# Attention's output norm in a macaron block: a head's inverse root as a zero-step stationary operand in four column groups, in place of a spread copy and its transposes

## The chip, the cores and the metric

The kernel runs on 1 core of one Trainium2 chip. The metric is the device time of one execution in microseconds (us), here the median of several runs. The engines are named as in the profile: PE is TensorE (PEld its weight loads), DVE is VectorE, ACT is ScalarE, POOL is GpSimd, SP is SyncE, which only issues transfers here.

## What is computed

A "macaron" block on x of shape (8, 512, 512), f32: half a feed-forward layer, attention, and half a feed-forward layer again. The feed-forward layer lets each of 16 experts choose its 256 best tokens; all experts share one 512x512 matrix. The attention has 16 heads of width 32 and 4 key heads, a second softmax over the difference of two, and a norm for each head. Cut to what matters:

```python
x = x + 0.5 * ffn(layernorm(x))
x = x + attn(layernorm(x))
x = x + 0.5 * ffn(layernorm(x))

def attn(x):
    ...
    diff = softmax(where(causal, NEG, scores[:, 0] - lam * scores[:, 1]))
    att = einsum('bhqv,bvhd->bqhd', diff, v)
    att = att * rsqrt(mean(att * att, axis=-1, keepdims=True) + EPS) * rms_w
    att = att * (1.0 - LAM_INIT)
    return att.reshape(b, s, E) @ Wo

def ffn(x):
    logits = xf @ router_w + router_b
    G, idx = top_k(softmax(logits, axis=-1).T, k)
    y = zeros.at[idx].add(G * (xf[idx] @ expert_w + expert_b))
    return y
```

The change is in the line with `rsqrt`: every token has 16 numbers, one for each head, and each must multiply the 32 values of its head.

## The kernel before, in words

The whole of x stays in SBUF, a batch of 512 tokens as four tiles of 128 tokens. The order of the work on every engine is written out by hand: each engine does its instructions in the order in which the program lists them, and waits only for what they need.

*Feed-forward, twice* (`ffn`, L213). A batch is normalised by POOL (`xn`, L254), transposed by PE (`tp`, L265), routed (`lgp`, L284, with the padded router weights `rwp` as a stationary operand of 32 columns in four column groups), and multiplied by the expert matrix (`yps`, L317); POOL adds the bias `eb` (L327). Then a search over 30 bits finds the threshold (`search`, L386, with the 0/1 masks `blk`, `low` and `seg`, which are slices of `sel`), and `update` (L451) adds the weighted result to x. Router weights, bias and masks are loaded once, at the start, into the pool `keep`, and are used by both layers.

*Attention* (`attention`, L460). For each batch there are two halves, `gp` 0 (called even here) and `gp` 1 (odd), and each half has 11 blocks: a block is a tile of 128 queries with some of the heads. The loop at L938 goes through all 176 blocks. In one turn `k` the engines work on five blocks at once: scores of block k+1 (`sc`, L655), energies with mask and row minimum (`e`, L672, on DVE), first exponentials (L685, on ACT), weights on POOL (`fac` L699, `e` L714, the causal fill L721) and the difference of the two softmaxes (`t`, L734, on DVE) for block k-1, second exponentials (L748) for k-2, transposes of `t` (`tp`, L768, copied out at L781 and L783), and the product with v for k-4 (`av`, L796, copied out at L811). The `av` matmuls have 32 stationary columns and stand at the column positions 0, 32, 64 and 96.

Beside the blocks, other work is put into *slots* of a turn: "short" and "long" for PE, "act mid" and "act" for ACT, "mid" and "dve" for DVE, "pool" for POOL. The pool slot comes last in a turn, and its first instruction waits for the difference `t` of that turn (L736). `plan` (L863) decides which work goes to which turn of a half:

- `norm_steps` (L467): in the even half of batch b, the norm of batch b+1. Statistics on DVE in turns 0 and 3, the inverse root on ACT in turn 4 (L480, L481), then on POOL the shift `nmr` = -mean x rstd as two instructions (L485, L486) and the normalised tile `h` (L488) in turns 6 to 9, the transposes `htp` (L496) in turns 7, 8 and 10. For batch 0 the same steps run before the blocks, while DVE still does the updates of the first feed-forward layer.
- `rope_steps` (L536): projections `r_ps` (L547) in turns 0 to 4, with two DVE instructions that read the PSUM bank (`r`, L556, and `r_by`, L558), two transfers on SP's queue for the swap (L564), and an addition on POOL (L568). `value_steps` (L515): `vps` (L523).
- `finish_steps` (L574): for each of a batch's four tiles, the head norm, the output projection and the residual. Tiles 0 and 1 are finished in the batch's odd half, tiles 2 and 3 in the next batch's even half, so 32 times in all.

The steps of `finish_steps`, with the turns of tiles 0, 1, 2 and 3 in their halves:

- POOL squares the attention output, `sq` (L583), and the second softmax's sum, `u` (L584); turns 4, 6, 0, 3.
- PE sums the squares over each head, `f_ss` (L590); DVE adds (L596); ACT takes the inverse root in two instructions (L601, L602). `u` then has 16 numbers for each of 128 tokens; turns 5, 7, 1, 5.
- POOL copies `u` out to 512 columns, each number 32 times, `f_ux` (L606); turns 5, 8, 1, 6.
- PE transposes it in four pieces into a PSUM bank, `f_f` (L614), and DVE multiplies with the attention output, `f_an` (L618); turns 7, 9, 4, 7.
- PE projects, `f_o` (L626), in turns 9, 10, 5, 8, and DVE adds to x (L632) a turn later.

`sq`, `f_ux` and `f_an` share two buffers of the tag "sq"; `h` has two buffers of its own. A new tile in a shared buffer waits until the last reader of the old one is through. The PSUM tiles of these steps, and `r_ps`, `vps`, `av` and `htp`, take turns in two banks (`MISC`).

In the last odd half (batch 7) there is no projection left; products of the second feed-forward layer take the "long" slots (`early_steps`, L888). Thirteen turns follow (`drain`, L1056), which finish tiles 2 and 3 of batch 7 beside that layer's first steps.

Of the kernel before, what the change touches and what calls it, by code (L numbers as in the profile page):

```python
# [9 lines left out]
F32 = mybir.dt.float32  # L10
I32 = mybir.dt.int32
AF = mybir.ActivationFunctionType
ALU = mybir.AluOpType
# [3 lines left out]
P = 128  # L17
B, S, E = 8, 512, 512
NT = B * S // P
TPB = S // P  # L20
EC = E // P
H, KVH, D = 16, 4, 32
R = H // KVH
NEXP = 16
# [9 lines left out]
C_BLK = C_SWAP + P  # L34
C_LOW = C_BLK + P
C_SEG = C_LOW + P
C_ALL = C_SEG + B
# [3 lines left out]
def macaron_kernel(  # L41
# [57 lines left out]
    eb_sb = keep.tile([P, E], F32, name="eb")  # L99
    sel = keep.tile([P, C_ALL - C_BLK], F32, name="sel")  # L100
    blk, low = sel[:, :P], sel[:, P : 2 * P]
    seg = sel[:, C_SEG - C_BLK : C_SEG - C_BLK + B]

    rwp = keep.tile([P, EC, 32], F32, name="rwp")
# [108 lines left out]
    def ffn(f):  # L213
# [5 lines left out]
        def new(kind, name, shape, dtype=F32, tag=None, **kw):  # L219
            return home[kind].tile(list(shape), dtype, name=f"{name}{f}", tag=tag or kind, **kw)  # L220

        def load():
            held["we"] = new("we", "we", [P, EC, E])
            nc.sync.dma_start(held["we"], expert_w.rearrange("(c p) n -> p c n", p=P))

# [53 lines left out]
        def logits_pe(b):  # L279

            lgps[b] = bank(at["lgp"], f"lgp{f}_{b}")
            xT = buf[b].rearrange("p i (c t) -> p c i t", c=EC)
            for c in range(EC):
                nc.tensor.matmul(  # L284
                    lgps[b][32 * c : 32 * (c + 1), :], rwp[:, c, :], xT[:, c], start=True,
                    stop=True, tile_position=(0, 32 * c),
                )
# [38 lines left out]
        def product_bias(b, i):  # L326
            return nc.gpsimd.tensor_tensor(buf[b][:, i, :], buf[b][:, i, :], eb_sb, ALU.add)  # L327
# [58 lines left out]
        def search(per_bit):  # L386

            softmax(1)
# [13 lines left out]
            thr = tiny.tile([P, 1], I32, name=f"thr{f}", tag="thr")  # L402
# [20 lines left out]
            cg = tiny.tile([P, 1], F32, name=f"cg{f}", tag="cg")  # L423
            ce = tiny.tile([P, 1], F32, name=f"ce{f}", tag="ce")
# [11 lines left out]
            need = tiny.tile([P, 1], F32, name=f"need{f}", tag="need")  # L436
# [11 lines left out]
            held["wt"] = tiny.tile([P, TPB, B], F32, name=f"wt{f}", tag="wt")  # L448
# [11 lines left out]
    def attention(f0, f1, home, first_end, projections_end, drain):  # L460
# [6 lines left out]
        def norm_steps(at, b, st):  # L467

            mv = tiny.tile([P, TPB, 2], F32, name=f"mv{b}", tag="a_mv")
            rstd = tiny.tile([P, TPB], F32, name=f"rstd{b}", tag="a_rstd")  # L470
            nmr = tiny.tile([P, TPB], F32, name=f"nmr{b}", tag="a_nmr")
# [10 lines left out]

            def apply(i):
                if i == 0:
                    nc.gpsimd.tensor_tensor(nmr, mv[:, :, 0], rstd, ALU.mult)  # L485
                    nc.gpsimd.tensor_scalar(nmr, nmr, -1.0, None, ALU.mult)  # L486
                hs[i] = home["h"].tile([P, E], F32, name=f"h{b}_{i}", tag="h", bufs=2)
                return nc.gpsimd.tensor_scalar(  # L488
                    hs[i], x_sb[b][:, i, :], rstd[:, i : i + 1], nmr[:, i : i + 1],
                    ALU.mult, ALU.add,  # L490
                )
# [21 lines left out]
            at(4, "act", scale)  # L513

# [59 lines left out]
        def finish_steps(at, os, b, i, st):  # L574
# [29 lines left out]
            def spread():  # L604
                t["ux"] = home["sq"].tile([P, 4, P], F32, name=f"{name}_ux", tag="sq", bufs=2)
                return nc.gpsimd.tensor_copy(  # L606
                    t["ux"].rearrange("p c (h d) -> p (c h) d", d=D),
                    t["u"].unsqueeze(2).to_broadcast([P, H, D]),
                )

            def turn():
                t["f"] = misc(f"{name}_f")
                for c in range(4):
                    nc.tensor.transpose(t["f"][:, c * P : (c + 1) * P], t["ux"][:, c, :], ident)  # L614
# [24 lines left out]
            at(o2, "pool", spread)  # L639
# [355 lines left out]
    CHOICE = ("st", "gt", "eq", "rank")  # L995
# [10 lines left out]
    nc.vector.memset(rwp, 0.0)  # L1006
    nc.sync.dma_start(rwp[:, :, :NEXP], router_w.rearrange("(c p) n -> p c n", p=P))
# [3 lines left out]
    nc.sync.dma_start(eb_sb, expert_b.partition_broadcast(P))  # L1011
    nc.sync.dma_start(sel, consts[:, C_BLK:])
# [19 lines left out]
    home = dict.fromkeys(("h", "hT", "kq0", "by", "sw"), proj)  # L1032
    opened = {}

    def first_end():
        first_y.close()
        opened["out"], opened["blocks"] = pool("out", "right"), pool("blocks", "right")
        home.update(dict.fromkeys(("aT", "sq"), opened["out"]))
        home.update(dict.fromkeys(("kq1", "v", "e", "t", "eT"), opened["blocks"]))

    def projections_end():
        proj.close()
        wpool.close()
        opened["early"] = pool("early", "left")
        f1.home.update(dict.fromkeys([*Y[:3], "we", *SMALL], opened["early"]))
        f1.at.update(tp=MISC, y=MISC, lgp=MISC, lg=MISC)
        f1.load()

    def blocks_end():
        opened["blocks"].close()  # L1050
        opened["late"] = pool("late", "right")
        f1.home.update(dict.fromkeys([*Y[3:], *CHOICE], opened["late"]))

# [107 lines left out]
```

## Time and profile before

| | |
|---|---|
| median of 4 runs | 1505.92 us (1505.64, 1506.2, 1513.32, 1496.21) |
| the profiled execution | 1505.64 us |
| its span, first to last instruction | 1503.9 us |
| mean granted PE clock | 0.936 of full |
| `f_f` (L614), PE | 128 records, 21.1 us busy, 17.1 us idle before |
| `f_ux` (L606), POOL | 32 x 0.61 us, 19.6 us busy |
| `av` (L796) 128x32 by 128x128, PE | 2304 records, 88.8 us busy |
| `nmr` (L485 and L486), POOL | 8 and 8, 2.1 and 3.2 us busy |
| `h` (L488), POOL | 32, 28.5 us busy |
| HBM read and written | 16.43 MB and 8.39 MB |

How to read it: the profile names every instruction by its line, its engine and its tile (`f_f`, `h`), with its start in us from the first instruction. "Busy" times of PE overlap, for matmuls are pipelined, so sums on PE come from the chain of waits, where steps follow each other. The number in brackets behind an instruction is the time for which its engine sat idle before it, with the instruction that ended the wait; of several semaphores the one that came last is named, and where the named one had long been done it was another. An f32 matmul shows as two records, a transpose as one.

### The profile page before, as it was taken

Reading aid. Unit: us, or ns where it says so; the run is one execution under the profiler, and the core shown is the slowest. Engines: PE = TensorE matmul, PEld = TensorE weight load, DVE = VectorE, ACT = ScalarE, POOL = GpSimd, SP = SyncE. Lnnn points to the kernel's source line nnn. Section 1 sums busy time; section 2 is a strip of 40 time slices with the busy share of each in tenths; the row PEclk is TensorE's granted clock in tenths of the full one; section 3 lists DMA queues with packets and bytes.
Section 4 is the critical chain, followed back from the end, with each engine's and each line's share of the span. In section 5 each row is a group of like instructions: output and inputs, shape, how many; then the busy total and the mean of one; then the engine's idle time right before and its main releaser. Section 6 shows DMA issues by size and latency. Waiting matters only on the chain.

```text
span 1503.9 us, 28143 instructions
## 1 busy us (share of the span) xinstructions
PE 1374.7 (91%) x8600; PEld 769.4 (51%) x8600; DVE 1197.3 (80%) x4425; ACT 1064.9 (71%) x3551; POOL 774.8 (52%) x1297
## 2 busy tenths in 40 slices
PE   5999799999999999999998999999999997999992
PEld 3544344555555555555554655555555544545551
DVE  4445679889979998998899799879988999744467
ACT  2411128988888898989898888978898989833210
POOL 5643436454645555564656455554656564645331
PEclk9999899899999999899999899999999998999996
DMA  9200010000000101000000000000000010000006
GB/s 349 62 0 1 0 43 29 15 22 15 22 30 8 37 1 36 4 34 15 22 23 15 29 9 36 1 29 8 36 8 29 16 50 2 1 0 1 1 1 223
DMA packets 25512, 47.61 MB, mean 32 GB/s; under 512 B 3968, under 2 KB 5136, under 8 KB 25360
## 3 DMA queue, kind: packets, MB, share of 16 engines
q1 hardware_dynamic: 21840, 36.88, 6.9%
q10 hardware_dynamic: 2400, 4.72, 0.8%
q0 software_dynamic: 1120, 4.20, 0.7%
q8 instruction: 68, 1.11, 0.3%
q14 instruction: 84, 0.69, 0.2%
HBM read 16.43 MB, written 8.39 MB: 17 GB/s over the span
## 4 chain that ended last, share of the span: by engine, by line
PE 68%; DVE 20%; POOL 7%; ACT 3%; issue 2%; DMA 1%; POOLq 0%; DVEq 0%; SPq 0%
PE r_ps L547 15%; PE yps L317 14%; PE sc L655 11%; PE f_o L626 8%; PE tp L768 6%; DVE t L734 6%; DVE e L672 5%; PE av L796 4%; PE f_ss L590 2%; PE tp L265 2%; DVE x L452 2%; ACT e L685 2%; POOL r L568 2%; PE vps L523 2%; POOL e L714 2%
## 5 line engine op out<-in xcount | busy, mean ns | idle before, releaser
L685 ACT ACTIVATE e<-e,nb 128x512 f32<-128x512 f32 (+3 forms) x1024 | 560.7, 551 | 8.8 <-DVE nb L672 3.6
L672 DVE CUSTOM_DVE_ANT_0 e<-sc,mpos 128x512 f32<-128x512 f32 (+3 forms) x1024 | 434.7, 486 | 21.0 <-PE sc L655 13.5
L748 ACT ACTIVATE t<-t,nm 128x512 f32<-128x512 f32 (+3 forms) x512 | 282.2, 554 | 71.0 <-DVE nm L734 70.4
L714 POOL TENSOR_SCALAR e<-e,z,fac 128x512 f32<-128x512 f32 (+3 forms) x512 | 306.5, 612 | 18.4
L655 PE MATMUL sc<-r,r 32*128 32x256 f32 (+3 forms) x2048 | 285.0, 503 | 11.7 <-DVE nb L672 8.3
L734 DVE CUSTOM_DVE_ANT_0 t<-e,fac 128x512 f32<-128x512 f32 (+3 forms) x512 | 254.7, 546 | 13.2 <-POOL e L721 12.5
L317 PE MATMUL yps<-we,y 128*128 128x512 f32 x512 | 246.3, 611 | 0.0
L547 PE MATMUL r_ps<-hT,wq_sb 128*128 128x512 f32 x512 | 239.4, 612 | 0.0
L768 PEld LDWEIGHTS tp<-ident,t 128*128 128x128 f32 x1280 | 153.7, 148 | 116.7 <-issue 38.3
L768 PE MATMUL tp<-ident,t 128*128 128x128 f32 x1280 | 190.7, 290 | 7.6 <-ACT eT L783 6.5
L685 ACT ACTIVATION_READ_ACCUMULATOR e<-e,nb 128x1 f32 x1024 | 194.2, 190 | 0.0
L655 PEld LDWEIGHTS sc<-r,r 32*128 32x128 f32 x2048 | 131.0, 202 | 82.5 <-DVE nb L672 57.7
L568 POOL TENSOR_TENSOR r<-r,r_sw 128x512 f32<-128x512 f32 x80 | 101.6, 1279 | 138.2 <-DVE z L692 75.3
L327 POOL TENSOR_TENSOR y<-y,eb 128x512 f32<-128x512 f32 x64 | 81.7, 1276 | 161.5 <-ACT y L324 137.1
L547 PEld LDWEIGHTS r_ps<-hT,wq_sb 128*128 128x128 f32 x512 | 95.3, 193 | 125.6 <-issue 107.5
L324 ACT COPY y<-yps 128x512 f32<-128x512 f32 x64 | 37.4, 585 | 152.6 <-PE yps L317 149.0
L781 DVE COPY eT<-tp 128x512 f32<-128x512 f32 (+1 forms) x176 | 111.9, 636 | 28.1 <-PE tp L768 28.1
L699 POOL TENSOR_TENSOR fac<-z,nlm 128x4 f32<-128x4 f32 (+2 forms) x176 | 37.1, 211 | 186.8 <-DVE z L692 186.8
L317 PEld LDWEIGHTS yps<-we,y 128*128 128x128 f32 x512 | 89.4, 192 | 85.1 <-issue 81.8
L626 PE MATMUL f_o<-wo_sb,f_an 128*128 128x512 f32 x256 | 123.1, 625 | 0.0
L783 ACT COPY eT<-tp 128x512 f32<-128x512 f32 (+1 forms) x176 | 94.1, 534 | 26.7 <-PE tp L768 26.0
L721 POOL TENSOR_SCALAR_AFFINE_SELECT e<-e 128x256 f32<-128x256 f32 (+1 forms) x224 | 96.5, 441 | 9.4
(111 smaller groups left out, 1637.5 us busy)
## 6 DMA issues: line engine op xcount, KB each, us to landing
r_sw<-r_by SPq DMA_DIRECT2D x160, 128.0 KB, 2.0
x<-in_x_dram POOLq DMA_DIRECT2D x4, 1024.0 KB, 15.7
out_dram<-x ACTq DMA_DIRECT2D x4, 1024.0 KB, 4.7
x<-in_x_dram SPq DMA_DIRECT2D x3, 1024.0 KB, 22.7
out_dram<-x SPq DMA_DIRECT2D x3, 1024.0 KB, 4.6
we<-in_expert_w_dram SPq DMA_DIRECT2D x2, 1024.0 KB, 7.3
wq_sb<-in_wq_dram SPq DMA_DIRECT2D x1, 2048.0 KB, 14.9
x<-in_x_dram SPq DMA_DIRECT2D x4, 256.0 KB, 4.2
```

What stands on the lines that cost most here:

```text
L317: nc.tensor.matmul(held["yps"], buf[b][:, i, c * P : (c + 1) * P], held["we"][:, c, :], start=(c == 0), stop=(c == EC - 1),)
L547: nc.tensor.matmul(t["ps"], w[:, c, c0 : c0 + P], st["hT"][:, c, :], start=(c == 0), stop=(c == EC - 1),)
L568: return nc.gpsimd.tensor_add(out, out, t["sw"])
L626: nc.tensor.matmul(t["o"], t["an"][:, c, :], wo_sb[:, c // 2, c % 2, :], start=(c == 0), stop=(c == 3),)
L655: nc.tensor.matmul(u["sc"][j][:, r * n : (r + 1) * n], kq[1 + head][j * D : (j + 1) * D, i * P : (i + 1) * P], kq[0][j * D : (j + 1) * D, ...
L672: nc.vector.tensor_tensor_reduce(out=u["e"][:, j, r * n : (r + 1) * n], in0=u["sc"][j][:, r * n : (r + 1) * n], in1=mpos[:, S - n :], scal ...
L685: nc.scalar.activation(e, e, AF.Exp, bias=u["nb"][:, c : c + 1], scale=-1.0, accum_out=u["z"][:, 0, c : c + 1],)
L714: nc.gpsimd.tensor_scalar(e, e, u["z"][:, 1, c : c + 1], u["fac"][:, 0, par, r : r + 1], ALU.mult, ALU.mult,)
L734: u["diff"] = nc.vector.tensor_tensor_reduce(out=u["t"][:, par, s], in0=u["e"][:, 2 * par, s], in1=u["e"][:, 2 * par + 1, s], scale=u["fac ...
L748: nc.scalar.activation(t, t, AF.Exp, bias=u["nm"][:, par, r : r + 1], scale=-1.0, accum_out=z2[:, col : col + 1],)
L768: nc.tensor.transpose(u["tp"][par][:, o : o + P], u["t"][:, par, r * n + c * P : r * n + (c + 1) * P], ident,)
L781: nc.vector.tensor_copy(o, s)
```

## The change

The copy `f_ux` goes. The transpose of 128 tokens by 128 columns of it is replaced by four matmuls: the stationary operand is one column of `u`, read 32 times with a step of zero (128x32), the moving operand is the identity, and the result is that head's inverse root in 32 partitions and 128 token columns. A tile needs 16 such matmuls, at the column positions 0, 32, 64 and 96 in turn, in place of four transposes.

With it come smaller edits. The shift `nmr` moves from POOL (two instructions, turn 6) to DVE (one instruction, turn 5). `h` gives up its own two buffers: it shares those of `sw` before the blocks, and later those of `sq` and `f_an`. Some small tiles go from two buffers to one. Router weights, bias and masks leave `keep` and are loaded by each feed-forward layer anew, into its own pools: for the second layer the router weights (with a memset on DVE), the expert matrix and the bias at the start of the last odd half, the masks in the drain.

The order of instructions on each engine is otherwise as before: 384 matmuls more on PE, on POOL 32 copies and 16 small instructions less, on DVE 8 shifts and one memset more, on SP's queue three transfers more, none on ACT. Where a shared buffer is taken, the tile pool gives the one that was released first: within a batch `h` 0 follows `sq` of tile 3, `h` 1 follows `h` 0, `h` 2 follows `h` 1, and `h` 3 follows `f_an` of tile 3.

```diff
-            def spread():
-                t["ux"] = home["sq"].tile([P, 4, P], F32, name=f"{name}_ux", tag="sq", bufs=2)
-                return nc.gpsimd.tensor_copy(
-                    t["ux"].rearrange("p c (h d) -> p (c h) d", d=D),
-                    t["u"].unsqueeze(2).to_broadcast([P, H, D]),
-                )
-
             def turn():
                 t["f"] = misc(f"{name}_f")
                 for c in range(4):
-                    nc.tensor.transpose(t["f"][:, c * P : (c + 1) * P], t["ux"][:, c, :], ident)
+                    for q in range(4):
+
+                        nc.tensor.matmul(
+                            t["f"][q * D : (q + 1) * D, c * P : (c + 1) * P],
+                            t["u"][:, 4 * c + q : 4 * c + q + 1].to_broadcast([P, D]), ident,
+                            start=True, stop=True, tile_position=(0, q * D),
+                        )
...
-            at(o2, "pool", spread)
...
+            def shift():
+                nc.vector.scalar_tensor_tensor(
+                    nmr, mv[:, :, 0], -1.0, rstd, ALU.mult, ALU.mult
+                )
+
             def apply(i):
-                if i == 0:
-                    nc.gpsimd.tensor_tensor(nmr, mv[:, :, 0], rstd, ALU.mult)
-                    nc.gpsimd.tensor_scalar(nmr, nmr, -1.0, None, ALU.mult)
-                hs[i] = home["h"].tile([P, E], F32, name=f"h{b}_{i}", tag="h", bufs=2)
+                where, tag = home["h"]
+                hs[i] = where.tile([P, E], F32, name=f"h{b}_{i}", tag=tag, bufs=2)
...
             at(4, "act", scale)
+            at(5, "mid", shift)
...
         def load():
             held["we"] = new("we", "we", [P, EC, E])
+
+            held["rwp"] = new("we", "rwp", [P, EC, 32], tag="rwp")
+            nc.vector.memset(held["rwp"], 0.0)
+            nc.sync.dma_start(
+                held["rwp"][:, :, :NEXP], router_w.rearrange("(c p) n -> p c n", p=P)
+            )
             nc.sync.dma_start(held["we"], expert_w.rearrange("(c p) n -> p c n", p=P))
+
+        def load_bias():
+            held["eb"] = new("we", "eb", [P, E], tag="eb")
+            nc.sync.dma_start(held["eb"], expert_b.partition_broadcast(P))
+
+        def load_choice():
+            held["sel"] = new("sel", "sel", [P, C_ALL - C_BLK])
+            nc.sync.dma_start(held["sel"], consts[:, C_BLK:])
...
-    home = dict.fromkeys(("h", "hT", "kq0", "by", "sw"), proj)
+    home = dict(
+        hT=proj, kq0=proj, by=proj, sw=proj, h=(proj, "sw")
+    )
...
-        home.update(dict.fromkeys(("aT", "sq"), opened["out"]))
+        home.update(aT=opened["out"], sq=opened["out"], h=(opened["out"], "sq"))
...
         f1.load()
+        f1.load_bias()
...
+        f1.load_choice()
```

## The prediction

> **What bounds the kernel now.** I read the page first (engines, chain), then the matmuls by form, the chain in order of time, the timeline around one batch's four `f_f` blocks (tiles 0 and 1 of a batch are finished in the odd half, tiles 2 and 3 in the next even half; a half is 11 turns), and last the busy time by stretch.
>
> ```profile
> PE 1374.7 (91%) x8600; PEld 769.4 (51%) x8600; DVE 1197.3 (80%) x4425; ACT 1064.9 (71%) x3551; POOL 774.8 (52%) x1297
> ...
> PE 68%; DVE 20%; POOL 7%; ACT 3%; issue 2%; DMA 1%; POOLq 0%; DVEq 0%; SPq 0%
> ```
>
> ```profile
> 523.00:554.00 31.00, 27.87 (x216) 15.88 (x216) 29.97 (x98) 28.92 (x85) 20.12 (x36) 1.00 0.03 10
> ```
>
> TensorE (PE) carries 68% of the chain, but not all of the time: from 523 to 554 us VectorE (DVE) is busy for 29.97 of 31 us and PE for 27.87 (the columns after the length are PE, weight loads, DVE, ScalarE, POOL, clock). In the rope turns of a half PE runs without a gap; in the later turns, where `f_f` lies, DVE sets the pace. So each `f_f` must be judged at its own place.
>
> ```profile
> 501.41 1.01 PE av L796 x32
> ...
> 1314.00 0.44 PE f_f L614 x4
> ```
>
> ```profile
> 174.82 0.65 POOL L485 TENSOR_TENSOR nmr<-mv,rstd 128x4 f32<-128x4 f32 x1
> ...
> 176.25 6.83 POOL L488 TENSOR_SCALAR h<-x,rstd,nmr 128x512 f32<-128x512 f32 x4
> 178.59 1.12 PE L496 MATMUL htp<-ident,h 128*128 128x128 f32 x4 [6.25 <-POOL h L488]
> ...
> 463.27 0.63 POOL L606 COPY f_ux<-f_u 128x512 f32<-128x512 f32 x1 [1.50 <-DVE z L692]
> ...
> 465.55 0.41 POOL L721 TENSOR_SCALAR_AFFINE_SELECT e<-e 128x256 f32<-128x256 f32 x1
> 465.67 0.28 DVE L811 COPY aT<-av 128x128 f32<-128x128 f32 x1
> ...
> 466.00 0.62 DVE L734 CUSTOM_DVE_ANT_0 t<-e,fac 128x384 f32<-128x384 f32 x1
> ...
> 467.24 0.60 PE L614 MATMUL f_f<-ident,f_ux 128*128 128x128 f32 x4
> ...
> 469.57 1.05 PE L590 MATMUL f_ss<-hsum,f_sq 128*128 128x4 f32 x8 [1.73 <-POOL f_sq L583]
> ...
> 478.46 0.66 PE L614 MATMUL f_f<-ident,f_ux 128*128 128x128 f32 x4 [0.67 <-POOL f_ux L606]
> ...
> 480.70 0.68 DVE L618 TENSOR_TENSOR f_an<-aT,f_f 128x512 f32<-128x512 f32 x1
> ...
> 481.42 3.70 PE L626 MATMUL f_o<-wo_sb,f_an 128*128 128x512 f32 x8
> ...
> 522.28 0.68 DVE L558 SCALAR_TENSOR_TENSOR r_by<-r_ps,cst 128x512 f32<-128x512 f32 x1
> ...
> 523.11 0.63 PE L614 MATMUL f_f<-ident,f_ux 128*128 128x128 f32 x4 [1.82 <-POOL e L714]
> ...
> 523.48 0.41 DVE L811 COPY aT<-av 128x256 f32<-128x256 f32 x1
> ...
> 523.81 0.68 DVE L618 TENSOR_TENSOR f_an<-aT,f_f 128x512 f32<-128x512 f32 x1
> ...
> 536.52 0.66 PE L614 MATMUL f_f<-ident,f_ux 128*128 128x128 f32 x4
> ...
> 537.10 1.71 PE L655 MATMUL sc<-r,r 32*128 32x512 f32 x8
> ```
>
> The first fence is from the chain of waits (start, us, engine, tile, line, records), the second from the timeline, where the bracket is the engine's idle time and what ended it. It shows the start of attention, then one batch's `f_f` for tiles 0, 1, 2 and 3, with what stands around each.
>
> **Price of the new block.** Four transposes of 128 columns cost 0.44 us of PE in steady state. They become 16 matmuls, 128x32 stationary, 128 moving columns, at column positions 0, 32, 64, 96. The nearest row is `av`: 16 matmuls of this very shape at the same four positions, 32 records (an f32 matmul shows two, a transpose one) in 1.01 us. So +0.57 us for each of the 32 tiles, 18.2 us of PE. What no row shows is a stationary operand of zero step. Lower bound: no slower than `av`, 1.01. Upper bound: no overlap between the groups, 32 records at a transpose's steady 0.44/4 = 0.11, 3.5 us. I take 1.01, for the shape, type and positions are `av`'s and only the read step differs.
>
> The Trainium skill's "TensorE: Matmul & The Clock Gate", Part 3, has three column tiles gain 2.38 times and not 3, at 512 columns. With that loss, 8 rounds of 0.11 us become 0.88 x 3/2.38 = 1.1 us by estimate, about 1 us more in the sum. `av`'s 1.01 is the loss measured in this very case, and I go by it.
>
> **Tile by tile, what of the 0.57 us reaches the end.**
> - Tile 0 (467.24): PE then waits 1.73 us for POOL's `f_sq`. The 0.57 lies in that wait: 0. If the cover went (`f_sq` 1.2 us sooner), 0.57 x 7 = 4 us.
> - Tile 1 (478.46): the block ends its 0.67 us wait for `f_ux`, so it starts near 477.8 and ends near 478.8 instead of 479.05. What follows is gated by DVE: the scores' banks are freed by the energies, and `f_o` starts at 481.42, when `f_an` (480.70 plus 0.68) has ended. 0. One of the seven (615.44, 0.85 us on the chain, so about half clock) has no wait to remove and PE is late after it: 2.0 for 0.85, and I count +1.0.
> - Tile 2 (523.11): PE idles 1.82 us before it. The row names POOL, whose copy was long done; the wait is for the PSUM bank that `r_by` (522.28 plus 0.68) still reads, so it stays. Then DVE is free for `f_an` at 523.48 + 0.41 = 523.89, but a block of 1.08 (with its tail, as `av` shows in the timeline) ends at 524.19: `f_an` starts 0.43 later than 523.81. DVE is full here, so this passes on. Five batches at 0.43; two (795.92 and 935.86, 0.85 and 0.84 us) ran at about half clock and wait for the block already: +1.2 each. Together 4.55.
> - Tile 3 (536.52): the scores after it take 1.71 us, because DVE frees their fourth bank at 537.6; unhindered such a group takes 1.07. Starting 0.57 later, they end at 537.67 + 1.07 = 538.74, as before. 0.
> - Batch 7: products fill every gap of PE. Tiles 0, 1 and 3 (1299.54, 1314.00, 1371.44 in the chain) pay 3 x 0.57 = 1.7; at tile 2 (1355.84) the chain runs through DVE's statistics: 0.
>
> **POOL's copy goes** (32 x 0.61 = 19.6 us of POOL). The chain holds 14 of them, 8.6 us. But look at tile 0: the POOL work behind the copy ends at 465.55 + 0.41 = 465.96, while DVE's `aT` ends at 465.67 + 0.28 = 465.95, and the difference `t` starts at 466.00. DVE is next, 0.01 us behind. At tile 1 the select ends at 480.70 and DVE reaches `t` only at 481.30. So 0; the bound on the other side is -8.6.
>
> **The shift `nmr`** leaves POOL (two instructions) and becomes one on DVE, in turn 5 after the energies. In the batches POOL was idle there and `h` waits for the difference anyway: 0 gained. On DVE it is 0.16 us (median of the same instruction at L240), in front of `eT`'s copy and a `t` that waits 0.44 us for POOL (529.02): 0; without that cover 7 x 0.16 = 1.1 us. Its own wait, for `rstd`, ended 3.7 us before. At the start it is different: the two instructions fill 174.82 to 176.25 ahead of the first `h`, and PE idles 6.25 us for it. DVE makes the shift between updates before POOL is through with its bias at 174.8, so `h` comes up to 1.4 us sooner: -1.3.
>
> **Buffers.** `h` shares two buffers with `sq` and `an`. `h` 1 and 2 now wait for the transpose of the `h` before, which ended 3 us ahead of them (536.6 for 539.88, 541.7 for 544.64); `h` 3 waits for `f_o` of tile 3, which ends at 547.1, and started at 549.97: 2.9 us of slack, 0. Single small buffers: last readers are a batch back, 0.
>
> **Transfers.** Router weights, bias and choice masks are loaded a second time. On SP's queue the 32 KB of router weights, behind a DVE memset of 0.165 us, go ahead of the expert weights (issued at 1216.98, landing 8.8 us at most; first use 1287.77, 71 us later), the bias behind them. The masks wait for the last blocks' buffers, go out near 1355 and are read at 1411.79; they took 13.9 us in the crowded start. No other load stands behind them. 0.
>
> **Sum.** +1.0 + 4.55 + 1.7 - 1.3 = +5.95 on the profiled execution's 1505.64 us (span 1503.9, 1.7 around it) makes 1511.6. That execution lies 0.3 under the median of 1505.92; so 1512.
>
> **Rivals.**
> - *PE's added time is paid everywhere.* For it: 68% of the chain. Against: the waits of 1.73, 0.67 and 1.82 us. 18.2 - 1.3 gives 1523, slower by 1.1%; it decides if 29 of 32 blocks pay.
> - *The column groups do not overlap with a zero-step operand* (ends slower). At 3.5 us a block, beyond the cover: tiles 2 and 3 pay 2.5 more, tile 1 0.95, tile 0 1.3, in seven batches, and batch 7 7.4; +58, so 1570. It decides from about 1.6 us a block. Against it: `av`.
> - *POOL's relief is real*: all 14 copies on the chain come off: 1512 - 8.6 = 1503. Against: DVE 0.01 us behind at tile 0.
> - *The clock rises.* The granted clock was 1.00 from 738 to 758 us and 0.77 from 601 to 623. Tile 0's copies follow each other by 136.42, 136.39, 139.55, 141.46 and 139.02 us; if all took 136.4, 10.8 us go: 1501. Against: copy of tile 0 to copy of tile 1 took 14.53 us at 1.00 (736.08 to 750.61) and 14.53 at the low clock (599.69 to 614.22): where the new matmuls stand, the clock hardly counts.
>
> The same page of the skill, Part 4, says that transposes don't count as busy for the clock gate as matmuls do. That speaks for this rival, and the sum by it would be the 1501 just given; no run here shows it yet.
>
> **How the numbers follow.** Mine 0.65; paid everywhere 0.13; no overlap 0.06; POOL's relief 0.08; clock 0.08. About 1% (15 us: under 1491, over 1521) is what a measurement here can tell from no change, for the four runs of before span 1496 to 1513. Faster: a tenth of mine is spread over both sides, most of it slower, and a part of the clock's: 0.05. Slower: no overlap, two thirds of "paid everywhere", a little of mine: 0.17. Same: 0.78. The range takes in both gains (1501, less the spread of runs) and "paid everywhere": 1496 to 1526.
>
> **What would show it.** `f_f` as 32 records in 1.0 to 1.1 us; PE's wait before `f_ss` down from 1.73 to about 1.2; `f_an` of tile 2 starting with the end of `f_f`; no L606 and still no earlier `t` at tile 0; the first `h` near 174.9; `h` waiting for no `f_o`. I am wrong if blocks take over 1.6 us, if turns 0 to 3 of a half shrink with a higher clock, or if the batch period drops below 136.

## The result and the profile after

The changed kernel takes 1495.08 us (median of 53 runs) beside 1502.78 us for the kernel before (79 runs): a ratio of 0.9958, 95% interval 0.9945 to 0.9971; the ratio is taken over the fast runs and is not the quotient of the two medians (0.9949). I forecast +0.4%; it is -0.4%, and 1495 lies just under the range's lower end, 1496. The profiled execution took 1494.84 us, its span is 1493.1 us against 1503.9, its mean granted clock 0.943 against 0.936.

From the page of the changed kernel, engines and chain:

```profile
PE 1378.2 (92%) x9496; PEld 778.7 (52%) x9496; DVE 1198.2 (80%) x4434; ACT 1062.6 (71%) x3551; POOL 751.5 (50%) x1249
...
PE 66%; DVE 25%; ACT 3%; POOL 3%; issue 2%; DMA 1%; DVEq 0%; SPq 0%; POOLq 0%; ACTq 0%
```

PE is busy for 3.5 us more than before, DVE carries 25% of the chain where it carried 20%, and POOL has nearly left it (7% to 3%). The timeline of the changed kernel at the places that the prediction showed: the start of attention, tiles 0 and 1 of a batch, tiles 2 and 3 (behind the start, everything runs 5 to 8 us ahead of before):

```profile
175.33 1.30 POOL L336 TENSOR_TENSOR y<-y,eb 128x512 f32<-128x512 f32 x1 [2.63 <-ACT y L333]
...
176.75 6.76 POOL L502 TENSOR_SCALAR h<-x,rstd,nmr 128x512 f32<-128x512 f32 x4
178.51 1.11 PE L510 MATMUL htp<-ident,h 128*128 128x128 f32 x4 [4.40 <-POOL h L502]
...
457.61 0.41 POOL L734 TENSOR_SCALAR_AFFINE_SELECT e<-e 128x256 f32<-128x256 f32 x1
458.27 0.28 DVE L824 COPY aT<-av 128x128 f32<-128x128 f32 x1
458.47 0.61 DVE L747 CUSTOM_DVE_ANT_0 t<-e,fac 128x384 f32<-128x384 f32 x1
459.94 1.08 PE L624 MATMUL f_f<-ident,f_u 128*32 128x128 f32 x32
...
462.05 1.05 PE L605 MATMUL f_ss<-hsum,f_sq 128*128 128x4 f32 x8 [1.02 <-POOL f_sq L598]
...
470.19 1.08 PE L624 MATMUL f_f<-ident,f_u 128*32 128x128 f32 x32
...
473.18 0.68 DVE L632 TENSOR_TENSOR f_an<-aT,f_f 128x512 f32<-128x512 f32 x1
...
514.83 0.68 DVE L573 SCALAR_TENSOR_TENSOR r_by<-r_ps,cst 128x512 f32<-128x512 f32 x1
...
515.57 1.08 PE L624 MATMUL f_f<-ident,f_u 128*32 128x128 f32 x32 [1.73 <-DVE r_by L573]
...
516.03 0.42 DVE L824 COPY aT<-av 128x256 f32<-128x256 f32 x1
516.72 0.69 DVE L632 TENSOR_TENSOR f_an<-aT,f_f 128x512 f32<-128x512 f32 x1 [0.27 <-PE f_f L624]
...
531.29 1.08 PE L624 MATMUL f_f<-ident,f_u 128*32 128x128 f32 x32
532.30 1.25 PE L668 MATMUL sc<-r,r 32*128 32x512 f32 x8
```

Nearly all of the steps came as described: the block is 32 records in 1.08 us; the wait ahead of `f_ss` shrinks from 1.73 to 1.02 us; at tile 0 POOL now ends 0.53 us ahead of DVE's `aT` (before, 0.01 us behind it), and `t` starts 0.20 us behind the start of `aT` instead of 0.33; tile 2's `f_an` waits for the block; the first `h` follows POOL's bias at once (0.12 us behind its end, 1.39 before). So the sum should have been about right, and yet the sign is wrong.

Where the time went in these two executions is seen in the groups of PE (and DVE's `r`) between the first energies of batch 0 and those of the last half, 1038.6 us before and 1025.0 after (columns: busy and mean of one, then idle time ahead and who ended it). Before, then after:

```profile
L547 PE MATMUL r_ps<-hT,wq_sb 128*128 128x512 f32 x480 | 225.5, 613 | 0.0
...
L547 PE MATMUL r_ps<-hT,wk_sb 128*128 128x512 f32 x120 | 70.3, 739 | 0.0
...
L590 PE MATMUL f_ss<-hsum,f_sq 128*128 128x4 f32 x224 | 30.2, 258 | 12.3 <-POOL f_sq L583 12.1
...
L614 PE MATMUL f_f<-ident,f_ux 128*128 128x128 f32 x112 | 18.6, 291 | 17.1 <-POOL e L714 12.7 <-POOL f_ux L606 4.4
...
L556 DVE SCALAR_TENSOR_TENSOR r<-r_ps,cst 128x512 f32<-128x512 f32 x75 | 51.6, 688 | 29.5 <-PE r_ps L547 29.5
```

```profile
L562 PE MATMUL r_ps<-hT,wq_sb 128*128 128x512 f32 x480 | 223.9, 610 | 0.0
...
L562 PE MATMUL r_ps<-hT,wk_sb 128*128 128x512 f32 x120 | 62.7, 671 | 0.0
...
L624 PE MATMUL f_f<-ident,f_u 128*32 128x128 f32 x896 | 31.1, 281 | 12.0 <-DVE r_by L573 12.0
L605 PE MATMUL f_ss<-hsum,f_sq 128*128 128x4 f32 x224 | 29.3, 254 | 7.3 <-POOL f_sq L598 7.2
...
L571 DVE SCALAR_TENSOR_TENSOR r<-r_ps,cst 128x512 f32<-128x512 f32 x75 | 51.5, 687 | 17.8 <-PE r_ps L562 17.6
```

`f_f` costs PE 12.5 us more in these 28 tiles, and PE's idle time falls by 12.6 us (59.4 to 46.8; the two brackets of `f_ss` and `f_f` give 10.1 of it): in the sums, the added work is covered. What is left is that matmuls which nobody changed got shorter: the projections `r_ps` by 9.2 us of busy time and the scores `sc` by 6.8 (267.2 to 260.4 over their four shapes), with `f_o` 2.0 longer. Same shape, same count, other duration: that is the clock. It reaches DVE, whose wait for `r_ps` (the last line of each fence) falls from 29.5 to 17.8 us. The batches by stretch, the first and then the next six, before and after (last columns: granted clock, DMA share, GB/s):

```profile
210.70:351.20 140.50, 131.01 (x794) 71.37 (x795) 117.16 (x466) 117.63 (x409) 72.02 (x132) 0.88 0.06 20
351.20:1181.50 830.30, 782.88 (x5569) 452.10 (x5568) 744.14 (x2893) 731.00 (x2528) 465.19 (x852) 0.94 0.06 20
```

```profile
212.20:344.80 132.60, 126.20 (x850) 71.06 (x851) 116.95 (x467) 116.97 (x409) 70.25 (x128) 0.91 0.06 21
344.80:1170.80 826.00, 787.62 (x6241) 457.33 (x6240) 744.26 (x2899) 729.46 (x2528) 448.49 (x816) 0.95 0.06 21
```

Of the 12 us, 8 lie in the first batch, and there the first `f_f` comes only 111 us after the first energies (118 before), so 6 of the 8 are gone before any new block. Its clock is 0.91 instead of 0.88 at the same work of DVE (117 us). So the clock must be looked at window by window.

**What the clock does.** In every trace of this study the granted clock is full or half, and it changes only on a grid of 3.413 us that is fixed within an execution and lies differently in the next. Stretches cut along this grid in batch 0, the second of each pair at half speed, before and after:

```profile
229.60:233.00 3.40, 3.40 (x10) 1.56 (x11) 3.40 (x17) 3.40 (x15) 2.18 (x5) 1.00 0.01 2
233.00:236.40 3.40, 3.40 (x5) 1.35 (x4) 3.30 (x15) 3.40 (x15) 2.13 (x2) 0.50 0.01 2
```

```profile
249.10:252.50 3.40, 2.88 (x15) 1.48 (x11) 3.04 (x12) 3.39 (x11) 2.92 (x5) 1.00 0.02 2
252.50:266.20 13.70, 13.59 (x78) 8.39 (x79) 12.47 (x45) 12.76 (x39) 8.70 (x15) 0.50 0.00 0
```

Before, the half-speed window falls on the projections `r_ps` (five records, PE busy 3.40 of 3.40 us, back to back). The eight records there take 5.40 us, and DVE waits 1.36 us for them; the same eight take 3.70 us in the changed kernel, at full speed, and DVE does not wait:

```profile
232.25 5.40 PE L547 MATMUL r_ps<-hT,wq_sb 128*128 128x512 f32 x8
...
237.69 0.69 DVE L556 SCALAR_TENSOR_TENSOR r<-r_ps,cst 128x512 f32<-128x512 f32 x1 [1.36 <-PE r_ps L547]
```

```profile
234.23 3.70 PE L562 MATMUL r_ps<-hT,wq_sb 128*128 128x512 f32 x8
...
238.22 0.69 DVE L571 SCALAR_TENSOR_TENSOR r<-r_ps,cst 128x512 f32<-128x512 f32 x1
```

After, four half-speed windows in a row fall on the late turns, where DVE is busy for 12.47 of 13.7 us and sets the pace anyway. The mean clock tells how many windows there are; the time depends on where they lie. Between the first energies of batch 0 and of the last half, counted from the trace's clock and matmul records, the profile before has 39 half-speed windows and 40.2 us of `r_ps` in them, the changed one 30 and 21.4 us. Half of that difference, 9.4 us, is the 9.2 us by which the projections got shorter.

How far this carries is seen from all twenty profiles of this study (the runs e1 to e18 are described below). Take off the same stretch half of the half-speed time in which PE runs `r_ps` or `f_o`, of which there are 28 to 54 us; these two were picked after the fact, because PE hardly waits ahead of them. Three profiles with the old block and the old shift (before, e13, e15) are then left with 1013.3 to 1014.2 us, though the stretch itself takes them 1031.0 to 1038.6. Eleven with the new block (changed, e1, e4, e5, e6, e9, e10, e11, e14, e16, e18) are left with 1007.5 to 1009.1, though it takes them 1024.8 to 1034.1. The others: e8, e12 and e17 1004.5 to 1005.8, e3 1011.2, e7 1015.0, e2 1016.3. So half speed on these two is paid at half its time, whichever kernel it is, and some 5 us more go with the new block, by a path that no run separates.

The projections' 9.2 us, though, are luck of the two executions. In a second pair (e15 is the kernel before, e18 the changed one) the half-speed windows hold 28.9 us of `r_ps` before and 33.2 after, DVE waits 23.7 and 23.4 us for it, and the changed kernel's stretch is still 2.6 us shorter.

### The profile page after: what moved, and what is told of

The parts are those of the page before. It is cut to its first block, busy times and chain, and to the rows that moved or that the text cites. A ratio compares the mean times of both kernels' runs of the same rounds, so it can differ in the third digit from the quotient of the medians.

```text
span 1493.1 us, 29857 instructions
## 1 busy us (share of the span) xinstructions
PE 1378.2 (92%) x9496; PEld 778.7 (52%) x9496; DVE 1198.2 (80%) x4434; ACT 1062.6 (71%) x3551; POOL 751.5 (50%) x1249
## 4 chain that ended last, share of the span: by engine, by line
PE 66%; DVE 25%; ACT 3%; POOL 3%; issue 2%; DMA 1%; DVEq 0%; SPq 0%; POOLq 0%; ACTq 0%
PE yps L326 14%; PE r_ps L562 14%; PE sc L668 10%; DVE e L685 9%; PE f_o L640 8%; DVE t L747 6%; PE tp L781 6%; PE av L809 4%; PE tp L274 2%; ACT e L698 2%; DVE x L463 2%; PE f_ss L605 2%; PE vps L538 2%; DVE eT L794 2%; PE f_f L624 1%
## 5 line engine op out<-in xcount | busy, mean ns | idle before, releaser
L668 PE MATMUL sc<-r,r 32*128 32x256 f32 (+3 forms) x2048 | 279.3, 491 | 10.2 <-DVE nb L685 7.3
L747 DVE CUSTOM_DVE_ANT_0 t<-e,fac 128x512 f32<-128x512 f32 (+3 forms) x512 | 254.8, 546 | 13.8 <-POOL e L734 13.7
```

What stands on the lines that cost most here:

```text
L668: nc.tensor.matmul(u["sc"][j][:, r * n : (r + 1) * n], kq[1 + head][j * D : (j + 1) * D, i * P : (i + 1) * P], kq[0][j * D : (j + 1) * D, ...
L747: u["diff"] = nc.vector.tensor_tensor_reduce(out=u["t"][:, par, s], in0=u["e"][:, 2 * par, s], in1=u["e"][:, 2 * par + 1, s], scale=u["fac ...
```

## The experiments

Theories: **A**, the new block puts more PE work into its windows and fewer of them are followed by half speed. **B**, POOL's relief from the copy is real. **C**, the gain is in the rest of the change (shift, buffers, loads). **D**, where attention's start lies on the clock's grid decides what the first batch takes. Medians of 12 timed runs each; ratio to the kernel before on the same chip; mean clock over the timed runs (before 0.938, changed 0.943); "grid" is the time from batch 0's first energies to the next step of the clock's grid, and "first" and "next six" the batches' lengths, all three from the one profile.

| run | us | ratio, 95% interval | clock | grid | first | next six |
|---|---|---|---|---|---|---|
| before | 1502.8 | 1 | 0.938 | 1.83 | 140.6 | 830.2 |
| changed | 1495.1 | 0.9958 [0.9945, 0.9971] | 0.943 | 2.81 | 132.7 | 825.9 |
| e1 block alone | 1501.8 | 0.9984 [0.9954, 1.0014] | 0.945 | 1.91 | 138.8 | 825.7 |
| e2 all but the block | 1500.0 | 0.9967 [0.9940, 0.9995] | 0.940 | 2.95 | 132.8 | 841.7 |
| e3 true matmuls | 1503.5 | 0.9981 [0.9956, 1.0007] | 0.943 | 1.87 | 138.9 | 832.9 |
| e4 copy kept | 1496.3 | 0.9952 [0.9925, 0.9979] | 0.946 | 2.41 | 132.6 | 825.8 |
| e5 start later, two | 1495.1 | 0.9957 [0.9925, 0.9990] | 0.943 | 2.71 | 132.6 | 826.2 |
| e6 start later, five | 1498.0 | 0.9980 [0.9949, 1.0010] | 0.943 | 1.48 | 138.5 | 829.2 |
| e7 block twice | 1507.6 | 1.0029 [1.0002, 1.0056] | 0.953 | 1.37 | 137.8 | 829.4 |
| e8 block and shift | 1495.1 | 0.9943 [0.9912, 0.9974] | 0.945 | 2.23 | 132.3 | 821.8 |
| e9 first shift on POOL | 1501.2 | 0.9995 [0.9968, 1.0021] | 0.942 | 2.51 | 132.8 | 825.7 |
| e10 later shifts on POOL | 1499.9 | 0.9982 [0.9945, 1.0019] | 0.944 | 3.02 | 133.1 | 829.0 |
| e11 tile 0 twice | 1497.0 | 0.9971 [0.9943, 0.9999] | 0.952 | 2.96 | 132.7 | 826.2 |
| e12 tile 0 and htp | 1490.3 | 0.9931 [0.9898, 0.9965] | 0.957 | 2.18 | 132.3 | 822.5 |
| e13 before, later start | 1501.1 | 0.9982 [0.9946, 1.0018] | 0.939 | 2.64 | 132.7 | 836.3 |
| e14 block, later start | 1500.4 | 0.9953 [0.9921, 0.9984] | 0.947 | 3.00 | 132.7 | 829.7 |
| e15 before, again | 1502.5 | one run | | 2.02 | 134.0 | 831.0 |
| e16 block alone, again | 1501.7 | one run | | 2.59 | 132.5 | 832.9 |
| e17 htp only | 1493.7 | 0.9941 [0.9911, 0.9970] | 0.951 | 3.06 | 132.8 | 819.5 |
| e18 changed again | 1494.5 | 0.9938 [0.9910, 0.9966] | 0.945 | 2.88 | 132.7 | 829.3 |

**Which part is it: the first four.** e1 is the kernel before with the new `turn` and without `spread`; e2 is its counterpart, the changed kernel with the old two and `h` in buffers of its own. e3 keeps the copy:

```
-                    nc.tensor.transpose(t["f"][:, c * P : (c + 1) * P], t["ux"][:, c, :], ident)
+                    nc.tensor.matmul(t["f"][:, c * P : (c + 1) * P], t["ux"][:, c, :], ident,
+                                     start=True, stop=True)
```

and e4 is the changed kernel with POOL's copy still made, into a buffer that nobody reads.

> The kernel before with only the new block: 16 matmuls from the zero-step root, no spread copy on POOL; nmr, h's buffers and the loads as before. Theory A (the clock: 32 records of true matmuls with no wait for POOL in place of 4 transposes make fewer half-clock windows): ratio 0.995 to 0.997 of before, mean clock 0.941 to 0.944 against 0.936 to 0.938. Theory B (POOL's relief shortens the work itself): the same 0.995 to 0.997, but at before's clock, so that time times clock falls by 0.4%. Theory C (nothing comes from the block; the gain is the shift, the sooner first h and the buffers): 1.003 by my old sum, clock as before.

> The changed kernel with the old spread copy and transposes put back, and h in buffers of its own as before; what stays of the change is nmr on DVE, the second loads and the small buffers. Theories A and B: 0.999 of before (the first h 1.3 us sooner), clock 0.936 to 0.938. Theory C: 0.995 to 0.997.

> The kernel before, the copy kept, and its four transposes of the spread root made four plain matmuls against the same identity (8 records of 128 columns): PE works longer on the same wait pattern. Theory A in its strong form (true matmuls count for the clock where transposes do not): clock 0.939 or more, ratio 0.998 or less. If it is the waits that count and not the kind of matmul: 1.000 to 1.002, clock 0.936 to 0.938.

> The changed kernel with the spread copy still done by POOL at its old place, into a buffer that nobody reads; PE and DVE as changed. Theory A: like the changed kernel, 0.995 to 0.997 of before, clock 0.941 to 0.944. Theory B: the gain is lost, 1.000 to 1.003.

B falls. e4's copies are all there and its time is the changed kernel's:

```profile
L621 POOL COPY f_ux<-f_u 128x512 f32<-128x512 f32 x32 | 19.5, 610 | 63.2 <-DVE z L713 58.5 <-ACT f_u L617 4.8
```

19.5 us of POOL cost no more than the medians can tell, 1.2 us. They were not quite free: in the turn of tile 0, `t` starts 0.33 us behind the start of `aT` before, 0.30 to 0.32 in e4 and 0.20 in the changed kernel, in each of the seven batches, so the copy's price there is about 0.9 us. A holds for the clock, which rises with either kind of added PE work (e1 0.945, e3 0.943), but not for the time: neither e1 nor e3 is told from the kernel before. e1's profile has 29 half-speed windows, one less than the changed kernel's, but 38.2 us of `r_ps` still lie in them. C isn't it alone either: e2 gains 0.3%, at before's clock. The two ratios' product, 0.9951, is the changed kernel's within the error, so block and rest both have a share, and the block's own by the medians (0.16%) isn't told from nothing, nor from the 5 us that go with it in the profiles.

**The start and the grid.** e5 and e6 put idle POOL instructions ahead of the very first `h` of the changed kernel (two, five); e8 adds to e1 only `nmr` on DVE.

```
+                if b == 0 and i == 0:
+                    idle = tiny.tile([P, TPB], F32, name="idle", tag="idle", bufs=1)
+                    for _ in range(2):
+                        nc.gpsimd.tensor_tensor(idle, mv[:, :, 0], rstd, ALU.mult)
```

> The changed kernel with two extra small POOL instructions (0.65 us each, their result unused) ahead of the very first h, once: attention starts 1.3 us later, as in the kernel before. In the traces so far the first batch (first scores' energies of batch 0 to those of batch 1) took 132.6 to 132.8 us in the three kernels with the sooner first h and 138.8 to 140.5 in the three without. Theory D (where the work lies on the clock's grid of 3.41 us decides the first batch): back to 138 to 140.5 us, ratio 0.999 to 1.001 of before. If the sooner h is worth only itself: 133 to 134 us, +1.3 us on the changed kernel, ratio 0.996 to 0.997.

> The same with five extra instructions, 3.3 us, close to one whole step of the clock's grid. Theory D: the first batch is short again, 132 to 134 us, and the ratio is 0.997 to 0.999, so 2 to 5 us better than with two instructions. If lateness itself lengthens the first batch: 139 us or more, ratio 1.001 or more.

> The kernel before with two parts of the change: the new block without the copy, and nmr on DVE. h's own buffers, the loads and the small buffers as before. If these two parts are the gain: first batch 132 to 134 us, ratio 0.995 to 0.997, clock 0.942 or more. If the shared buffers or the loads carry a part of it: 0.998.

e8 says that block and shift are enough (28 half-speed windows, with 12.4 us of `r_ps` in them, and a span of 1488.7 us, where e1 with 29 and 38.2 us has 1499.7); shared buffers, loads and small buffers carry nothing that shows. The expected sizes of e5 and e6 missed, both times: the first batch was short with two instructions and long with five. Part of it is that the two delayed the first `h` by 0.6 us only (from the search's weights `wt` to `h` 9.3 us, 8.7 in the changed kernel, 10.0 before). The other part is that a profile is one execution, and each has its own grid. Read by the "grid" column the profiles agree with D: 1.37 to 1.91 us goes with 137.8 to 140.6 us, 2.18 and more with 132.3 to 133.1, whichever kernel it is.

So the shift was put back on POOL by halves, for the first batch (e9) and for the other seven (e10), and, to tell grid from work, three idle instructions were put ahead of the first `h` of the kernel before (e13) and of e1 (e14), which makes the start 1.9 us later on the clock's face 1.5 us sooner. Two further profiles (e15, e16) tested the rule where it was not read from.

> The changed kernel with nmr made by POOL's two instructions again for the first batch only, so that the first h comes 1.3 us later; the seven other shifts stay on DVE. Theory D (the cut of the first batch by the clock's 3.41 us grid; long, 138 to 140.5 us, or short, 132 to 133): most runs fall to the long side, median 1499 to 1502 us, ratio 0.998 to 1.000. If the shift's place in the later batches is what counts: as the changed kernel, 0.995 to 0.997.

> The counterpart: nmr on DVE for the first batch, on POOL for the seven others. Theory D: as the changed kernel, 0.994 to 0.997, first batch 132 to 133 us. If the later shifts carry the gain: 0.998 to 1.000.

> The kernel before with three more small POOL instructions (result unused) ahead of the very first h: attention starts 1.9 to 2.1 us later and nothing else changes. Theory D: 2.0 us later is 1.4 us sooner on the clock's 3.41 us grid, as the changed kernel is, so the first batch is more often short (132 to 133 us) and the later start is more than paid back: ratio 0.996 to 0.999. If only the work counts: +2 us, ratio 1.001.

> The run with the new block alone (1501.8 us median), and the same three POOL instructions ahead of the first h. Theory D: 1496 to 1499 us though it starts 2 us later, ratio 0.995 to 0.997. If only the work counts: 1503 to 1504 us, ratio 1.000.

> The kernel before once more, one profile. In the fourteen profiles so far the time from batch 0's first energies to the next step of the clock's grid was 1.4 to 1.9 us where the first batch took 137.8 to 140.6 us, and 2.15 to 3.0 us where it took 132.3 to 133.1. Theory D: this profile falls to one of the two in the same way, whichever kernel it is. Against it: a first batch near 140 us at 2.2 to 3.0, or near 132.5 at 1.4 to 1.9.

> The kernel with the new block alone once more, one profile, with the same expectation as the look at the kernel before; its turns 4 to 8 of the even halves should again hold PE's wait of f_an for f_f, 0.4 us each.

e9's ratio loses the gain, as D had it (its interval reaches down to 0.9968, the changed kernel's up to 0.9971), though its one profile shows a short first batch (it took 1496.2 us, its fastest run). e10 should have kept the gain by D and its interval allows both; its runs fall into two heaps, five at 1493 to 1498 and five at 1506 to 1508. e14 starts later and is not slower, against the +2 us of work alone, but only four of its runs are as fast as D named or faster (1493 to 1496 us), the others lie at 1500 to 1504; e13 tells nothing. e15 lies on the edge (2.02 us, 134.0 us), e16 agrees. The rule for the first batch thus holds in 19 of 20 profiles, with e15 between; that it carries the shift's whole share is not shown: e16 has the short first batch and still takes 1501.7 us, for it gives 7 us back in the next six. The kernels with the old block took 830 to 842 us for these six (five profiles, e3's four matmuls among them), those with the new one 820 to 833 (fourteen, without e7).

**What a half-speed window costs.** e7 makes all blocks twice, e11 only tile 0's, e12 tile 0's and, in batches 1 to 7, the transposes of token tile 2 four times; e17 has the transposes only, and e18 is the changed kernel on e17's chip.

```
-                for c in range(4):
+                for c in (0, 1, 2, 3) * (2 if i == 0 else 1):
...
-                for c in range(EC):
+                for c in list(range(EC)) * (4 if i == 2 and b > 0 else 1):
```

> The changed kernel with the 16 matmuls of every f_f made twice into the same bank, 1 us of PE more in each of 32 tiles. Paid everywhere: +32 us on the changed kernel, ratio 1.016. By my tile-by-tile prices at an unchanged clock: about +13 us (tile 2 all of it, tiles 1 and 3 a part, tile 0 little), ratio 1.004. Theory A (PE work in these gaps keeps the clock up): clock 0.946 or more and ratio 0.998 to 1.001.

> The changed kernel with tile 0's 16 matmuls made twice (the other tiles once): 1.0 us of PE work that nobody needs, placed in PE's idle 1.0 us ahead of f_ss. Theory A: the half-clock window that follows this place in each batch (464.1, 600.7, 877.2, 1017.1 and 1153.6 us in the changed kernel) goes, clock 0.947 or more, 6 to 12 us less than the changed kernel, ratio 0.987 to 0.992. If the fill is paid for as it was with all 32 blocks doubled: 0.997 to 1.000.

> As the run before, and besides the four transposes of htp of token tile 2 made four times in batches 1 to 7, 1.3 us more of PE work in the 2.0 us for which PE waits for the bank of the next htp. Theory A, and transposes count for the clock as well: the window at the end of the even half (412.9, 549.5, 826.0, 1102.4 us in the changed kernel) goes too, another 4 to 12 us, ratio 0.980 to 0.988. If transposes do not count for the clock: no better than the run before, clock unchanged within 0.001.

> The changed kernel with only the four transposes of htp of token tile 2 made four times in batches 1 to 7 (tile 0's block once). In the run with both fills this work lay wholly inside PE's wait for the next htp's bank, which fell from 2.0 to 0.7 us. If a half-clock window at the end of the even half is what the changed kernel still loses, and this fill is what gained: 1488 to 1492 us, ratio 0.990 to 0.994 of before, 3 us or more under the changed kernel on the same chip. If the fill takes away only windows in which PE is not the limit, as tile 0's fill did: as the changed kernel, 0.995 to 0.997.

> The changed kernel itself again, on the same chip as the run with htp's fill: 0.9945 to 0.9971 of before, as measured first. First batch 132 to 134 us if its first energies lie 2.1 to 3.0 us before a step of the clock's grid, 138 to 141 us at 1.4 to 1.9.

e7 takes 12.5 us more than the changed kernel, about the +13 of the tile-by-tile prices, though its clock is at 0.953. e11 is the clearest. Its filling is free, as the first line shows (`f_ss` waited 7.3 us for POOL in the changed kernel), and it removes the window it was aimed at: the stretch of tiles 0 and 1 in the odd half of batch 2 (counted from 0), in the changed kernel and in e11:

```profile
L605 PE MATMUL f_ss<-hsum,f_sq 128*128 128x4 f32 x256 | 33.5, 254 | 1.2 <-POOL f_sq L598 0.5
```

```profile
590.50:612.50 22.00, 20.97 (x180) 12.45 (x180) 20.38 (x68) 19.97 (x59) 10.98 (x22) 0.77 0.03 13
```

```profile
590.00:612.00 22.00, 21.28 (x240) 13.27 (x239) 19.23 (x63) 18.31 (x57) 12.32 (x23) 1.00 0.04 13
```

The clock goes from 0.77 to 1.00 here and the time of the whole does not move (1497.0 against 1495.1 us). DVE sets the pace in these turns, and half-speed windows on them cost nothing that shows. The transposes of e17 fill the wait for the next `htp`'s bank (13.6 us in the changed kernel, 4.3 with them) and raise the clock as well:

```profile
L510 PE MATMUL htp<-ident,h 128*128 128x128 f32 x212 | 32.6, 296 | 13.9 <-POOL h L502 9.5 <-DVE aT L824 4.3
```

e17 and e18 are the same in time, so e12's 1490.3 us is not shown to beat the changed kernel.

## Why the prediction was wrong

**The block's price: right, a little high.** 1.08 us as forecast (1.01 to 1.1), but against 0.60 to 0.66 us of PE with which the transposes stand in the timeline, not their steady 0.44: +0.45 us a tile (12.5 us in 28). Column groups overlap with a zero-step operand as they do in `av`.

**Tiles 0 and 3: right.** The added work is matched by idle time that goes. **Tile 1: right but for its one term.** A single block ran at half speed (1.94 us, in batch 2) and holds `f_an` back by 0.46 us, where I had +1.0. **Tile 2: mechanism right, size high.** `f_an` waits for the block, 0.27 us in the batch shown instead of 0.43; over seven even halves the energies fall back by 2.2 us in this turn where I had 4.55. The two batches that I had priced at half speed, 1.2 us each, ran this block at full speed and lost under 0.2. **Batch 7: right.** From the last half's first energies to the end the changed kernel loses 1.3 us, forecast 1.7. **POOL's copy: nearly right.** I had 0; it is about -0.9 us, for the 0.01 us by which I had DVE behind was read from the end of `aT`, and `t` can start 0.08 us ahead of that (458.47 against 458.27 + 0.28 above). **Buffers and transfers: right**; no `h` waits for `f_o`.

**First `h`: right for `h`, high for the sum.** It comes 1.27 us sooner behind POOL's bias, but of this only 0.3 us arrives at the first energies, where I had 1.3. That it also moves attention on the clock's grid wasn't in the sum.

**The step that failed is the rival "the clock rises", and why it was put aside:** "where the new matmuls stand, the clock hardly counts". This is true of the place, and e11 shows it once more. I drew from it that the sum needs no term for the clock. But I had measured it from tile 0 to tile 1, where DVE sets the pace, and half speed there costs nothing that shows; it costs where PE sets the pace, half of its time on `r_ps` and `f_o`, and `r_ps` is 9.2 us shorter in the profiled pair. The two cases ought to have been weighed at the projections: the rows of before show `r_ps` at 613 and 739 ns where its fastest record takes 592, and the 40.2 us of it at half speed are by estimate 20 us lost: that was the size of what the clock could give, and no bound of mine. The sum of +5.95 us stands only at an unchanged clock. With the prices as measured (2.2 at tile 2, 0.5 at tile 1, 1.3 in batch 7, -0.3 for `h`, -0.9 for the copy) it is near +3. The span of the profiled pair falls by 10.8 us, so some 14 us lie outside the sum, and about 10 over all runs. Of the 14, half of the 15 us by which `r_ps` and `f_o` spend less time at half speed (50.0 to 35.0) is 7.5, which the second pair does not repeat. The rest goes with the block; that fewer half-speed windows on other work (83 us before, 67 after) make it is likely and not shown.

The Trainium skill, "TensorE: Matmul & The Clock Gate", Part 4, says that transposes don't count for the gate as matmuls do, and the prediction used it in favour of this rival. For the f32 transposes of this kernel the runs speak against the rule: transposes alone, added in e17, raised the mean clock from 0.945 to 0.951 on one chip.

**What stays open.** How the 0.4% is shared. The block alone, the shift in the first batch and the shifts in the later batches each seem to take 2 to 6 us, and they do not add up; an interval of 0.6% with twelve runs and one profile a kernel doesn't settle it. That half speed is paid where it meets `r_ps` and `f_o` is shown; which part of the change moves the windows by how much, and what makes up the 5 us that go with the block, is not.

## What to carry to other kernels

A small edit also moves everything behind it on the clock's grid, so below about 1% the sum of an edit is not the forecast: read how much longer the matmuls of one shape are than their fastest record, in the stretches where PE sets the pace, and put that much into the range on both sides. Judge a clock by where its slow windows lie, not by its mean: e11 raised it by 0.009 and gained nothing. And take several executions before explaining 5 us of 1500.

## What the runs showed of the hardware

- The clock's steps lie on one grid of 3.413 us through a whole execution, in all twenty traces. The Trainium skill, "TensorE: Matmul & The Clock Gate", Part 1, has a free-running window of 3413 ns, and the traces agree.
- Half speed follows a window with little work by PE, and no long idle time is needed. I took for each of 5544 full-speed windows from the first projection to the last half, over all twenty traces, the share of it for which PE ran (each record counted until the next one starts), with scores (32 of 128 rows in use) counted a quarter and `f_ss` not at all. Below 0.20 all 70 were followed by half speed, from 0.20 to 0.35 157 of 181, up to 0.50 199 of 731, and above 0.50 none of 4562. The window at 229.6 us shown above is such a case: PE was busy all of its 3.40 us, 2.7 us of it with scores, and half speed followed. With transposes counted as nothing the best threshold sorts 369 windows wrongly, with them counted 192; the weights are read off these traces, and no run was made to test them.
- Half speed costs half of its time on `r_ps` and `f_o`, and little that shows elsewhere: with that taken off, eleven profiles with the new block lie within 1.6 us (1007.5 to 1009.1) instead of 9.3, though their half-speed windows number 21 to 35.
- A stationary operand of zero step costs PE no more than an ordinary one: 0.281 us a record for `f_f`, 0.291 for `av`.
